# First stage of a convolution block: the generating vectors of its matrices are built with a group of channels on each partition

## The chip, the core and the metric

The kernel runs on one core of a Trainium2 chip. A core has five engines that run their own instruction queues side by side: TensorE (PE in the profile, with its weight loads listed as PEld), VectorE (DVE), ScalarE (ACT), GpSimd (POOL) and SyncE (SP), the last of which only issues transfers here. Transfers between DRAM and the on-chip memory run on 16 DMA engines. The metric is the device time of one execution in microseconds (us); the times given are medians of several executions.

## The reference, cut to what matters

The input is 16 images of 192 channels and 64 x 64 pixels, float32. Layer 0 normalizes over channels, projects to 384 channels, convolves half of them depthwise, runs four directional scans and a second depthwise convolution, gates, batch-normalizes and projects back; an MLP follows. Layer 1 is a depthwise convolution whose taps depend on the image.

```python
h = _ln2d(x, ln1_w, ln1_b)
pg = _conv1x1(h, in_proj_w, in_proj_b)
projected, gate = jnp.split(pg, 2, axis=1)
projected = _dwconv3(projected, dw_k)
scanned = _directional_scan(projected, decay_logits, mix_logits, input_scale)
local = _dwconv3(projected, le_k)
mixed = (scanned + local) * jax.nn.sigmoid(gate)
...
decay = jnp.clip(jax.nn.sigmoid(decay_logits), 0.05, 0.995)
mix = jax.nn.softmax(mix_logits, axis=0)
iscale = 1.0 + jnp.tanh(input_scale)
...
lr = _scan_axis(x * sc(iscale[0]), decay[0], -1)
```

The second stage of the kernel computes the depthwise convolutions and one axis of the scans as matrix products: for each channel it needs eight 64 x 64 Toeplitz matrices. Such a matrix is given by one vector of 127 numbers, its generating vector: the value depends on the difference of row and column only. Three vectors per channel (k = 0 to 2) hold the columns of `dw_k`, three (k = 3 to 5) those of `le_k`, one (k = 4) also the two exponential tails of the scans along that axis, and two (k = 6, 7) a single number, the gain of the scans along the other axis. The gain is softmax(mix) x (1 + tanh(input_scale)) x (1 - decay).

## The kernel before

Three stages follow each other. The first (to about 620 us) reads the images, normalizes them over channels and projects them; the second (to about 1,390 us) works channel by channel; the third runs the output projection, the MLP and layer 1.

The first stage runs 64 iterations `n`, each over a pair of images and eight rows. In iteration n, `load_a(n + 3)` issues the loads of a later input tile `xa`, three on SP's queue and three on POOL's (L471; four buffers). `store` (L536) and, at the start of a block, `store_first` (L530) issue the stores of the block before. PE then turns the next tile (12 transposes, L483) and runs the projection (24 products, L512, into two PSUM buffers per image). DVE and ACT each evict one half of the result (L517, L518), DVE takes the statistics of the next tile (L490, L491). Four iterations make a block. The evicted block lies in one of two buffers by turns, `stg` and `mid`, each there once. The stores of a block are spread over the four iterations of the next block, the last of them (`PARTS` entry 4, 192 KB each) issued in its fourth iteration; after that the block after next writes the same buffer again.

The order on every engine is the order of the program text. Small jobs are set beside the iterations: `beside(n, f, ...)` lists function f for the end of iteration n, behind that iteration's loads, stores, products and evictions on each engine.

The generating vectors are such small jobs. `decays` (before the loop) and `gains` (iteration 1) compute decay and gain with channels on 64 partitions in three parts (`dec`, `gain`: 64 x 3 x 4). For vector k, `vector(k)` on DVE clears a slot of 64 x 3 x 128 numbers and copies the few that are not zero; for k = 4, `runs(t)` in three iterations adds the exponential tails with a scan each. `positions(k)` turns the slot with three PE transposes into a PSUM bank (L403), which ACT copies to a tile `gt` with position on the partitions (L405). `store_vector(k, part)` writes it to DRAM, to `dv_d` (k < 3, two parts) or `lv_d` (four parts), each part in an iteration of its own, by turns on the queues of SP and POOL (L412, L416). In DRAM the layout is `dv_d[group][k][position][8 channels]` and `lv_d[group][half][k][position][4 channels]`, so a partition of `gt` is written in runs of 8 or 4 float32: 32 or 16 bytes. The vectors' iterations are 9, 11, 13, 15, 19, 24, 28 and 32; `positions` follows two later (five for k = 4), the parts one iteration after another behind it. From iteration 46 on `load_dm` and `load_lm` read the matrices back, each row of a matrix shifted by one position.

The slots and small tiles lie in the room of a weight tile `wf1` that is loaded in iteration 41 (`room`, `cut`).

Of the kernel before, what the change touches and what calls it, by code (L numbers as in the profile page):

```python
# [21 lines left out]
F32 = mybir.dt.float32  # L22
AF = mybir.ActivationFunctionType
ALU = mybir.AluOpType
# [31 lines left out]
def conv_block_kernel(ctx: ExitStack, tc: tile.TileContext, x, prm, w_in, w_out, w_fc1, b_fc1, w_fc2, w1, bn1, w2, out):  # L56
# [189 lines left out]
    with ExitStack() as stage:  # L246
# [11 lines left out]
        dcol, imp = cut(64, 1728, 64), cut(64, 1792, 64)  # L258
        indt, svt = cut(3, 1984, 128), cut(3, 2112, C)
        dec = ka.tile([64, 3, 4], F32, tag="dec", name="dec")  # L260
        gain = ka.tile([64, 3, 4], F32, tag="gain", name="gain")
        tmp = ka.tile([64, 3, 4], F32, tag="tmp", name="tmp")
        red = ka.tile([64, 3], F32, tag="red", name="red")
# [3 lines left out]
        gts = {}  # L267
# [19 lines left out]
        def decays():  # L287

            nc.scalar.activation(dec, pt3[lo, :, DEC:DEC + 4], AF.Sigmoid)
            nc.vector.tensor_scalar(dec, dec, 0.05, 0.995, ALU.max, ALU.min)  # L290
            nc.scalar.activation(tmp, pt3[lo, :, ISC:ISC + 4], AF.Tanh)
            nc.vector.tensor_scalar_add(tmp, tmp, 1.0)
            nc.vector.tensor_reduce(red, pt3[lo, :, MIX:MIX + 4], AX.X, ALU.max)
            for t in range(3):
                nc.vector.tensor_scalar(gain[:, t], pt3[lo, t, MIX:MIX + 4], red[:, t:t + 1], None, ALU.subtract)
            nc.scalar.activation(gain, gain, AF.Exp)

        def gains():
            nc.vector.tensor_reduce(red, gain, AX.X, ALU.add)
            nc.vector.reciprocal(red, red)  # L300
            nc.vector.tensor_mul(gain, gain, tmp)
            nc.vector.tensor_scalar(tmp, dec, -1.0, 1.0, ALU.mult, ALU.add)
            nc.vector.tensor_mul(gain, gain, tmp)
            for t in range(3):
                nc.vector.tensor_scalar_mul(gain[:, t], gain[:, t], red[:, t:t + 1])
# [69 lines left out]
        slot = lambda k: cut(64, 384 * (k % 2), 384).rearrange("p (t n) -> p t n", t=3)  # L375

        def vector(k):
            gv = slot(k)
            nc.vector.memset(gv, 0.0)
            if k < 3:  # L380
                nc.vector.tensor_copy(gv[:, :, 62:65], pt3[lo, :, DW + 3 * k:DW + 3 * k + 3])
            elif k < 6:
                le = pt3[lo, :, LE + 3 * (k - 3):LE + 3 * (k - 3) + 3]
                nc.vector.tensor_copy(gv[:, :, 62:65], le[:, :, ::-1])
            else:
                nc.vector.tensor_copy(gv[:, :, 63:64], gain[:, :, k - 4:k - 3])

        def runs(t):

            gv = slot(4)  # L390
            if t == 0:
                nc.vector.memset(imp, 0.0)
            for k, vec in ((0, gv[:, t, 63:127]), (1, gv[:, t, 63::-1])):
                run = cut(64, 1856 + 64 * k, 64)
                nc.vector.tensor_scalar_mul(dcol, ones[lo, 0:64], dec[:, t, k:k + 1])
                nc.vector.tensor_copy(imp[:, 0:1], gain[:, t, k:k + 1])
                nc.vector.tensor_tensor_scan(run, dcol, imp, 0.0, ALU.mult, ALU.add)
                nc.vector.tensor_add(vec, vec, run)

        def positions(k):  # L400
            pg = bank()
            for t in range(3):
                nc.tensor.transpose(pg[:, 64 * t:64 * t + 64], slot(k)[:, t], ident[lo, lo])  # L403
            gts[k] = ka.tile([128, C], F32, tag="gt", name="gt", bufs=4)
            nc.scalar.copy(gts[k], pg[:, 0:C])  # L405

        def store_vector(k, part):

            queue = (nc.sync, nc.gpsimd)[part % 2]
            if k < 3:  # L410
# [855 lines left out]
```

## Time and profile before

| | us |
|---|---|
| median of three executions | 3730.94 |
| lowest and highest of them | 3727.93, 3739.55 |
| the profiled execution | 3721.87 |
| span of the profiled execution, first to last instruction | 3720.1 |

| engine, whole span | busy us | share |
|---|---|---|
| PE | 3694.2 | 99% |
| DVE | 2699.1 | 73% |
| ACT | 1785.3 | 48% |
| POOL | 419.6 | 11% |

How to read the profile: a line of a timeline or of a group names the line of the kernel (L512), the engine, the operation and "output<-input", then how often. What stands in brackets, or after a bar, is the time for which the engine sat idle before it, and what released it. SPq and ACTq are those engines as issuers of transfers; POOL's transfers stand under POOL. The releaser of a wait for several things is inferred, and can be the wrong one of them. DMA shares are means over the 16 engines. Matmuls are pipelined and their ends are modelled, so a busy PE is not a PE at its peak: the distance from one start to the next says more than the busy share.

### The profile page before, as it was taken

What the parts mean: (1) busy time and instruction counts of PE and PEld (TensorE: products, weight loads), DVE (VectorE), ACT (ScalarE), POOL (GpSimd) and SP (SyncE); (2) the same over time, 40 slices, a digit from 0 to 9 for tenths busy, and PEclk for the clock granted to TensorE, in tenths of its full rate; (3) what the DMA queues carried; (4) which work ended last, traced back from release to release, by engine and by line L of the source; (5) the groups of instructions that cost most, each with busy time, mean ns of one, the idle gap of its engine ahead of it and who ended that gap; (6) DMA issues with size and microseconds to landing.
All of it is one profiled execution on the core that took longest, in us unless ns stands there. A gap on an engine that the chain in (4) does not pass through costs nothing.

```text
span 3720.1 us, 71189 instructions
## 1 busy us (share of the span) xinstructions
PE 3694.2 (99%) x30344; PEld 1644.7 (44%) x30344; DVE 2699.1 (73%) x4154; ACT 1785.3 (48%) x1947; POOL 419.6 (11%) x683
## 2 busy tenths in 40 slices
PE   9999999999999999999999999999999999999999
PEld 6665666555555533333333333333333333333333
DVE  7887776999999965557757757666765766675763
ACT  3443444888888843334434433434343443443433
POOL 2434332101111020000000000000000000000000
PEclk9999999999999999999999999999999999999999
DMA  7899997999999851112212222222222221221212
GB/s 169 243 249 233 269 286 248 302 293 283 280 285 271 233 101 36 42 44 69 79 50 69 71 65 68 63 63 65 72 57 60 75 71 44 78 75 44 69 38 74
DMA packets 310236, 491.76 MB, mean 132 GB/s; under 512 B 46672, under 2 KB 204704, under 8 KB 309920
## 3 DMA queue, kind: packets, MB, share of 16 engines
q1 hardware_dynamic: 252128, 296.19, 29.8%
q0 software_dynamic: 56896, 189.89, 18.9%
q8 instruction: 240, 3.93, 0.5%
q10 hardware_dynamic: 896, 1.12, 0.1%
q14 instruction: 76, 0.62, 0.1%
HBM read 284.91 MB, written 197.92 MB: 130 GB/s over the span
## 4 chain that ended last, share of the span: by engine, by line
PE 98%; DVE 1%; DMA 1%; ACT 0%; issue 0%; SPq 0%; POOL 0%; ACTq 0%
PE ps_f L981 27%; PE ps_f L835 27%; PE ps_pj L512 14%; PE ps_l L669 11%; PE ps_d L625 7%; PE ps_o L906 5%; PE ps_xt L483 2%; PE ps_o L899 2%; PE ps_o L937 1%; DMA xa<-in_x_dram 0%; PE ps_k L835 0%; PE ps_d L1068 0%; PE ps_i L1109 0%; DVE v L662 0%; DVE v L660 0%; DMA pg_d<-mid 0%
## 5 line engine op out<-in xcount | busy, mean ns | idle before, releaser
L983 ACT ACTIVATE gl<-ps_f,bf 128x1024 f32<-128x1024 f32 x384 | 427.6, 1114 | 1319.2 <-PE ps_f L981 1319.2
L981 PE MATMUL ps_f<-h,wf 64*64 64x512 f32 x9216 | 1033.3, 593 | 3.0 <-DVE h L969 1.8
L835 PE MATMUL ps_f<-gl,place 128*64 128x512 f32 x4608 | 1022.2, 592 | 0.0
L981 PEld LDWEIGHTS ps_f<-h,wf 64*64 64x64 f32 x9216 | 333.6, 133 | 688.4 <-issue 633.7
L835 PEld LDWEIGHTS ps_f<-gl,place 128*64 128x64 f32 x4608 | 334.2, 137 | 574.5 <-issue 533.4
L512 PE MATMUL ps_pj<-wi,xa 64*128 64x384 f32 x3072 | 515.4, 488 | 2.9 <-DVE stg L517 2.9
L949 DVE TENSOR_TENSOR h<-ximg,ps_o 128x768 f32<-128x768 f32 x126 | 114.5, 950 | 420.9 <-PE ps_o L906 412.6
L512 PEld LDWEIGHTS ps_pj<-wi,xa 64*128 64x128 f32 x3072 | 294.4, 187 | 195.4 <-issue 12.2
L912 DVE SCALAR_TENSOR_TENSOR ximg<-ps_o,pt,low 128x256 f32<-128x256 f32 x384 | 167.8, 479 | 262.7 <-PE ps_o L906 259.1
L65 DVE SCALAR_TENSOR_TENSOR o<-ximg,taps,o 128x1024 f32<-128x1024 f32 x261 | 334.7, 1282 | 9.3 <-ACT o L1040 2.6
L1044 POOL DMA_DIRECT2D out_dram<-o x168 | 87.9, 528 | 2067.5 <-DVE o L65 2064.7
L968 DVE RECIPROCAL rs<-rs 128x512 f32<-128x512 f32 x64 | 214.3, 3349 | 28.6 <-ACT rs L965 28.6
L660 DVE TENSOR_TENSOR_SCAN v<-tab,q 128x1024 f32<-128x1024 f32 x96 | 218.3, 2274 | 7.8 <-ACT tab L648 7.8
L662 DVE TENSOR_TENSOR_SCAN v<-tab,q 128x1024 f32<-128x1024 f32 x96 | 217.4, 2265 | 0.0
L648 ACT ACTIVATE tab<-mask,dec_b 128x1024 f32<-128x1024 f32 x192 | 209.4, 1142 | 0.0
L906 PE MATMUL ps_o<-low,wo 128*64 128x256 f32 x1536 | 209.0, 393 | 0.0
L518 ACT ACTIVATE stg<-ps_pj,rsa 128x384 f32<-128x384 f32 x128 | 120.0, 941 | 184.2 <-PE ps_pj L512 168.8
L518 ACT ACTIVATE mid<-ps_pj,rsa 128x384 f32<-128x384 f32 x128 | 119.9, 938 | 182.1 <-PE ps_pj L512 178.4
L490 DVE BATCH_NORM_STATS2 st<-ps_xt 128x6 f32<-128x192 f32 x512 | 173.0, 338 | 14.4 <-PE ps_xt L483 14.2
L239 DVE STREAM_TRANSPOSE low<-low 128x512 f32<-128x512 f32 x174 | 167.7, 1014 | 2.0 <-issue 0.3
L1001 DVE SCALAR_TENSOR_TENSOR ximg<-ps_f,pt,ximg 128x512 f32<-128x512 f32 x192 | 134.4, 749 | 40.2 <-PE ps_f L835 37.8
L471 POOL DMA_DIRECT2D xa<-in_x_dram x192 | 119.9, 630 | 354.8 <-PE ps_pj L512 284.3
(211 smaller groups left out, 4047.2 us busy)
## 6 DMA issues: line engine op xcount, KB each, us to landing
low<-in_x_dram SPq DMA_DIRECT2D x128, 384.0 KB
out_dram<-o POOLq DMA_DIRECT2D x168, 256.0 KB, 3.7
mid<-pg_d SPq DMA_DIRECT2D x8, 4096.0 KB
low<-mixed_d SPq DMA_DIRECT2D x116, 256.0 KB
low<-pg_d SPq DMA_DIRECT2D x7, 4096.0 KB
pg_o<-pg_d SPq DMA_DIRECT2D x7, 4096.0 KB
xa<-in_x_dram POOLq DMA_DIRECT2D x192, 128.0 KB, 5.9
xa<-in_x_dram SPq DMA_DIRECT2D x192, 128.0 KB
```

The costliest lines, as they stand in the source:

```text
L65: nc.vector.scalar_tensor_tensor(o, in0, scalar, in1, ALU.mult, ALU.add, **kw)
L512: nc.tensor.matmul(ps[i], pixels(n, t, g)[q], wi[q, t].rearrange("p g k c -> p (g k c)"), start=(t == 0), stop=(t == 2))
L518: nc.scalar.activation(stag[blk][1][:, :, j], ps[1], AF.Copy, scale=rs[:, g, 1:2])
L625: nc.tensor.matmul(dst(ps[o, ih]), mats[g % 2]["dm"][q, di + 1, :, ch], src(s["pg"][q, :, 0, ch]), start=(di == 0), stop=stop)
L660: nc.vector.tensor_tensor_scan(vf, tab, q, 0.0, ALU.mult, ALU.add)
L662: nc.vector.tensor_tensor_scan(vf[:, ::-1], tab[:, ::-1], q[:, ::-1], 0.0, ALU.mult, ALU.add)
L669: nc.tensor.matmul(dst(bst[k]["ps"][o, i]), lm_of(g)[q, m, :, c], src(q, ih), start=start, stop=stop)
L835: nc.tensor.matmul(ps[q], w(i), rhs(i), start=start, stop=stop)
L906: nc.tensor.matmul(ps[wh][q].rearrange("p (r w) -> p r w", w=32), wo[:, 64 * t:64 * t + 64], cols(rows(s["mx"][:, i]))[:, :, wh], start=fi ...
L968: nc.vector.reciprocal(rs, rs)
L981: nc.tensor.matmul(pf[o, i], wf1[q, t, m0:m0 + 64], s["h"][q, t], start=(t == 0), stop=(t == 2))
L983: nc.scalar.activation(gl, pf, AF.Gelu, bias=bf1[:, m:m + 1])
```

## The change

The vectors are built with one group of eight channels on each of 24 partitions, each partition holding all 128 positions in the order in which DRAM has them. The parameters are loaded a second time for this, as `ptg` (24 x 8 x 50, issued by ACT before the loop). `group_gains` computes decay and gain from it in that layout (part 0 before the loop, part 1 in iteration 1); `decays` keeps only the decay that `diagonals` needs, and `gains` is gone. A slot is 24 x 1024 numbers, on partitions 64 to 87 or 96 to 119. POOL clears it, DVE copies the numbers that are not zero, and for k = 4 `runs(i, d)` makes the exponential tails, in four iterations, with one scan over 256 numbers each. `positions` is gone: there are no transposes, no copies by ACT and no `gt`. `store_vector` writes a vector with one transfer: `dv_d` on SP's queue in runs of 4 KB, `lv_d` on POOL's queue in runs of 2 KB. The vectors' iterations are now 13, 14, 15, 16, 24, 32, 33, 34, with the store one iteration later (five for k = 4).

```diff
--- before.py
+++ after.py
@@ -255,16 +255,11 @@
         dg = cut(64, 768, 576).rearrange("p (t k n) -> p t k n", t=3, k=3)
         lnb = cut(64, 1344, 384).rearrange("p (t n) -> p t n", t=3)
         mean_w = cut(64, 0, 128)
-        dcol, imp = cut(64, 1728, 64), cut(64, 1792, 64)
         indt, svt = cut(3, 1984, 128), cut(3, 2112, C)
         dec = ka.tile([64, 3, 4], F32, tag="dec", name="dec")
-        gain = ka.tile([64, 3, 4], F32, tag="gain", name="gain")
-        tmp = ka.tile([64, 3, 4], F32, tag="tmp", name="tmp")
-        red = ka.tile([64, 3], F32, tag="red", name="red")
         bp = ka.tile([64, 3], F32, tag="bp", name="bp")
         sv = ka.tile([64, 3, 3, 3], F32, tag="sv", name="sv")
         ind = ka.tile([128, 3], F32, tag="ind", name="ind")
-        gts = {}
 
         def bank():
             return psa.tile([128, CH], F32, tag="pb", name="pb")
@@ -288,21 +283,6 @@
 
             nc.scalar.activation(dec, pt3[lo, :, DEC:DEC + 4], AF.Sigmoid)
             nc.vector.tensor_scalar(dec, dec, 0.05, 0.995, ALU.max, ALU.min)
-            nc.scalar.activation(tmp, pt3[lo, :, ISC:ISC + 4], AF.Tanh)
-            nc.vector.tensor_scalar_add(tmp, tmp, 1.0)
-            nc.vector.tensor_reduce(red, pt3[lo, :, MIX:MIX + 4], AX.X, ALU.max)
-            for t in range(3):
-                nc.vector.tensor_scalar(gain[:, t], pt3[lo, t, MIX:MIX + 4], red[:, t:t + 1], None, ALU.subtract)
-            nc.scalar.activation(gain, gain, AF.Exp)
-
-        def gains():
-            nc.vector.tensor_reduce(red, gain, AX.X, ALU.add)
-            nc.vector.reciprocal(red, red)
-            nc.vector.tensor_mul(gain, gain, tmp)
-            nc.vector.tensor_scalar(tmp, dec, -1.0, 1.0, ALU.mult, ALU.add)
-            nc.vector.tensor_mul(gain, gain, tmp)
-            for t in range(3):
-                nc.vector.tensor_scalar_mul(gain[:, t], gain[:, t], red[:, t:t + 1])
 
         def diagonals(t):
             for k, v in enumerate((pt3[lo, t, GTB:GTB + 1], dec[:, t, 2:3], dec[:, t, 3:4])):
@@ -372,49 +352,69 @@
             by_half(bias_q[:, k], pq[:, 0:C])
 
 
-        slot = lambda k: cut(64, 384 * (k % 2), 384).rearrange("p (t n) -> p t n", t=3)
+
+        GP = slice(64, 64 + NCG)
+        ptg = ka.tile([128, GC, NPRM], F32, tag="ptg", name="ptg")[GP]
+        decg, gaing, tmpg = (ka.tile([128, GC, 4], F32, tag=n_, name=n_)[GP] for n_ in ("decg", "gaing", "tmpg"))
+        redg = ka.tile([128, GC], F32, tag="redg", name="redg")[GP]
+        NV = 128 * GC
+        slots = (room[GP, 0:NV], room[96:96 + NCG, 0:NV])
+        HN = GC // 2 * HW
+        dcol, imp, run = (room[GP, NV + k * HN:NV + (k + 1) * HN].rearrange("g (c m) -> g c m", m=HW) for k in range(3))
+        by_pair = lambda v: v.rearrange("g (i c) n -> g i n c", i=2)
+        slot = lambda k: slots[k % 2].rearrange("g (i s c) -> g i s c", i=2, c=GC // 2)
+
+        def group_gains(part):
+
+            mix = ptg[:, :, MIX:MIX + 4]
+            if part == 0:
+                nc.scalar.activation(decg, ptg[:, :, DEC:DEC + 4], AF.Sigmoid)
+                nc.scalar.activation(tmpg, ptg[:, :, ISC:ISC + 4], AF.Tanh)
+                nc.vector.tensor_scalar(decg, decg, 0.05, 0.995, ALU.max, ALU.min)
+                nc.vector.tensor_scalar_add(tmpg, tmpg, 1.0)
+                nc.vector.tensor_reduce(redg, mix, AX.X, ALU.max)
+                nc.vector.tensor_sub(gaing, mix, redg.unsqueeze(2).broadcast_to([NCG, GC, 4]))
+                nc.scalar.activation(gaing, gaing, AF.Exp)
+            else:
+                nc.vector.tensor_reduce(redg, gaing, AX.X, ALU.add)
+                nc.vector.reciprocal(redg, redg)
+                nc.vector.tensor_mul(gaing, gaing, tmpg)
+                nc.vector.tensor_scalar(tmpg, decg, -1.0, 1.0, ALU.mult, ALU.add)
+                nc.vector.tensor_mul(gaing, gaing, tmpg)
+                nc.vector.tensor_mul(gaing, gaing, redg.unsqueeze(2).broadcast_to([NCG, GC, 4]))
 
         def vector(k):
-            gv = slot(k)
-            nc.vector.memset(gv, 0.0)
+            nc.gpsimd.memset(slots[k % 2], 0.0)
             if k < 3:
-                nc.vector.tensor_copy(gv[:, :, 62:65], pt3[lo, :, DW + 3 * k:DW + 3 * k + 3])
-            elif k < 6:
-                le = pt3[lo, :, LE + 3 * (k - 3):LE + 3 * (k - 3) + 3]
-                nc.vector.tensor_copy(gv[:, :, 62:65], le[:, :, ::-1])
+                nc.vector.tensor_copy(slots[k % 2].rearrange("g (s c) -> g s c", c=GC)[:, 62:65],
+                                      ptg[:, :, DW + 3 * k:DW + 3 * k + 3].rearrange("g c j -> g j c"))
+                return
+            for i in range(2):
+                gv, c = slot(k)[:, i], slice(i * (GC // 2), (i + 1) * (GC // 2))
+                if k < 6:
+                    le = ptg[:, c, LE + 3 * (k - 3):LE + 3 * (k - 3) + 3]
+                    nc.vector.tensor_copy(gv[:, 62:65], le[:, :, ::-1].rearrange("g c j -> g j c"))
+                else:
+                    nc.vector.tensor_copy(gv[:, 63:64], gaing[:, c, k - 4:k - 3].rearrange("g c j -> g j c"))
+
+        def runs(i, d):
+
+            gv, c = slot(4)[:, i], slice(i * (GC // 2), (i + 1) * (GC // 2))
+            nc.vector.memset(imp, 0.0)
+            nc.vector.tensor_copy(imp[:, :, 0:1], gaing[:, c, d:d + 1])
+            nc.vector.memset(dcol[:, :, 0:1], 0.0)
+            nc.vector.tensor_copy(dcol[:, :, 1:HW], decg[:, c, d:d + 1].broadcast_to([NCG, GC // 2, HW - 1]))
+            flat = lambda v: v.rearrange("g c m -> g (c m)")
+            nc.vector.tensor_tensor_scan(flat(run), flat(dcol), flat(imp), 0.0, ALU.mult, ALU.add)
+            vec = gv[:, 63:127] if d == 0 else gv[:, 63::-1]
+            nc.vector.tensor_add(vec, vec, run.rearrange("g c m -> g m c"))
+
+        def store_vector(k):
+            if k < 3:
+                nc.sync.dma_start(dv_d[:, k].rearrange("g s c -> g (s c)"), slots[k % 2])
             else:
-                nc.vector.tensor_copy(gv[:, :, 63:64], gain[:, :, k - 4:k - 3])
-
-        def runs(t):
-
-            gv = slot(4)
-            if t == 0:
-                nc.vector.memset(imp, 0.0)
-            for k, vec in ((0, gv[:, t, 63:127]), (1, gv[:, t, 63::-1])):
-                run = cut(64, 1856 + 64 * k, 64)
-                nc.vector.tensor_scalar_mul(dcol, ones[lo, 0:64], dec[:, t, k:k + 1])
-                nc.vector.tensor_copy(imp[:, 0:1], gain[:, t, k:k + 1])
-                nc.vector.tensor_tensor_scan(run, dcol, imp, 0.0, ALU.mult, ALU.add)
-                nc.vector.tensor_add(vec, vec, run)
-
-        def positions(k):
-            pg = bank()
-            for t in range(3):
-                nc.tensor.transpose(pg[:, 64 * t:64 * t + 64], slot(k)[:, t], ident[lo, lo])
-            gts[k] = ka.tile([128, C], F32, tag="gt", name="gt", bufs=4)
-            nc.scalar.copy(gts[k], pg[:, 0:C])
-
-        def store_vector(k, part):
-
-            queue = (nc.sync, nc.gpsimd)[part % 2]
-            if k < 3:
-                n = NCG // 2
-                queue.dma_start(dv_d[part * n:part * n + n, k].rearrange("g s c -> s g c"),
-                                  gts[k].rearrange("s (g c) -> s g c", c=GC)[:, part * n:part * n + n])
-            else:
-                n = NCG // 4
-                queue.dma_start(lv_d[part * n:part * n + n, :, k - 3].rearrange("g i s c -> s (g i) c"),
-                                  gts[k].rearrange("s (g c) -> s g c", c=GC // 2)[:, 2 * part * n:2 * part * n + 2 * n])
+                nc.gpsimd.dma_start(lv_d[:, :, k - 3].rearrange("g i s c -> g i (s c)"),
+                                    slots[k % 2].rearrange("g (i n) -> g i n", i=2))
 
 
         side = {}
@@ -422,7 +422,7 @@
         def beside(n, f, *args):
             side.setdefault(n, []).append((f, args))
 
-        beside(1, gains)
+        beside(1, group_gains, 1)
         for t in range(3):
             beside(2 + t, diagonals, t)
         beside(5, gate_bias)
@@ -434,15 +434,12 @@
         for k in range(3):
             beside(18 + 2 * k, sums_across, k)
             beside(19 + 2 * k, conv_bias, k)
-        for k, n in enumerate((9, 11, 13, 15, 19, 24, 28, 32)):
+        for k, n in enumerate((13, 14, 15, 16, 24, 32, 33, 34)):
             beside(n, vector, k)
             if k == 4:
-                for t in range(3):
-                    beside(n + 1 + t, runs, t)
-            end = n + (5 if k == 4 else 2)
-            beside(end, positions, k)
-            for part in range(2 if k < 3 else 4):
-                beside(end + 1 + part, store_vector, k, part)
+                for j in range(4):
+                    beside(n + 1 + j, runs, j // 2, j % 2)
+            beside(n + (5 if k == 4 else 1), store_vector, k)
         for k in (0, 1, 3, 4):
             beside(40 + k, load_weights, k)
         for i in range(2):
@@ -541,6 +538,7 @@
             v = src.rearrange("(t p) n -> p t n", p=64)
             nc.sync.dma_start(dst[HALF[0]], v)
             nc.scalar.dma_start(dst[HALF[1]], v)
+        nc.scalar.dma_start(ptg, prm.rearrange("(g c) n -> g c n", c=GC))
         nc.vector.memset(ones, 1.0)
 
         idle = bank()
@@ -558,6 +556,7 @@
         steps = projection_weights()
         next(steps)
         decays()
+        group_gains(0)
         next(steps)
         next(steps)
         turn(0)
```

## The prediction

> **What bounds the kernel now.** The page comes first: the engines' shares say which engine sets the time, the chain which of its lines.
>
> ```profile
> PE 3694.2 (99%) x30344; PEld 1644.7 (44%) x30344; DVE 2699.1 (73%) x4154; ACT 1785.3 (48%) x1947; POOL 419.6 (11%) x683
> ...
> DMA  7899997999999851112212222222222221221212
> ...
> DMA packets 310236, 491.76 MB, mean 132 GB/s; under 512 B 46672, under 2 KB 204704, under 8 KB 309920
> ...
> PE 98%; DVE 1%; DMA 1%; ACT 0%; issue 0%; SPq 0%; POOL 0%; ACTq 0%
> ```
>
> PE is the chain, and the DMA engines are full in the first 14 slices, the first stage among them. Work taken from DVE, ACT or a queue counts only where PE waits for it. So the second view is the timeline of PE over three iterations, of which the middle one has no transposes of a vector:
>
> ```profile
> 133.37 0.34 PE L403 MATMUL pb<-ident,wf 64*128 64x64 f32 x3
> 133.64 1.53 PE L483 MATMUL ps_xt<-ident,xa 128*128 128x128 f32 x12
> 135.10 8.01 PE L512 MATMUL ps_pj<-wi,xa 64*128 64x384 f32 x48
> 143.04 1.53 PE L483 MATMUL ps_xt<-ident,xa 128*128 128x128 f32 x12
> ```
>
> From one L483 to the next it is 143.04 - 133.64 = 9.40 us, and the same in nearly every iteration to 604 us: PE runs at its own pace, though the DMA engines are full. I listed all 62 distances for what stands above 9.40. The eight iterations with L403 take 9.57 or 9.58. The jobs of other kinds (L315 to L371) take theirs and stay. Three are not explained by PE's work: 9.71 from 114.35, 9.86 from 443.36, and one of 15.05 from 324.73 us. The timeline there (all engines), and SP's own before it:
>
> ```profile
> 305.89 13.19 SPq L471 DMA_DIRECT2D xa<-in_x_dram  x3
> 319.12 2.13 SPq L536 DMA_DIRECT2D pg_d<-stg  x2
> 321.42 3.32 SPq L471 DMA_DIRECT2D xa<-in_x_dram  x3
> 324.79 1.30 SPq L536 DMA_DIRECT2D pg_d<-stg  x2
> 326.39 0.37 SPq L416 DMA_DIRECT2D lv_d<-gt  x1
> ...
> 332.98 1.58 ACT L518 ACTIVATE stg<-ps_pj,rsa 128x384 f32<-128x384 f32 x2 [7.13 <-DMA pg_d<-mid]
> 333.11 0.86 DVE L517 TENSOR_SCALAR stg<-ps_pj,rsa 128x384 f32<-128x384 f32 x1 [4.93 <-DMA pg_d<-mid]
> ...
> 334.02 5.84 PE L512 MATMUL ps_pj<-wi,xa 64*128 64x384 f32 x24 [2.86 <-DVE stg L517]
> ```
>
> A new block begins there (iteration 32), and its first evictions write `stg`. They wait until the last store of the block that lay in it has landed. The profile names a store from `mid`, but what is overwritten is `stg`; its last store left SP only at 324.79 to 326.09, 7 us before. It was late because SP was late: its three loads of 305.89 took 13.19 us to issue. DVE and ACT stand, both PSUM buffers fill, and PE waits 2.86 us. The 24 products after that take 5.84 us instead of 4.14: the page by windows gives PE a granted clock of 0.91 in 320 to 340 us and 1.00 on either side.
>
> Around that time the vectors' stores stand in both queues. Each moves 96 or 48 KB in 1,536 runs of 32 or 16 bytes:
>
> ```profile
> L416 SPq DMA_DIRECT2D lv_d<-gt x10: 366/1452/2260, 199.2 to 388.2; - x10
> L416 POOL DMA_DIRECT2D lv_d<-gt x10: 1034/1075/1077, 203.3 to 391.3; - x10
> ...
> L412 SPq DMA_DIRECT2D dv_d<-gt x3: 1327/1563/2089, 142.6 to 179.5; - x3
> ...
> DMA to landing us min/median/max: 6.5/9.6/12.0
> ```
>
> Six in `dv_d` and 20 in `lv_d` make 26 x 1,536 = 39,936 packets, of 46,672 under 512 B in the whole execution. In 277 to 296 us, with two of them on SP and two on POOL, the DMA engines moved 184 GB/s at a share of 0.95; in 454 to 473 us, with none, 274 at 0.89.
>
> **What the Trainium skill says.** "DMA: Bandwidth & Descriptors", section Specifications: a transfer needs runs of 512 B or more for the full rate, and below that the engine reads, modifies and writes. The 184 against 274 GB/s agree. The same page, "Issuing engines are not separate DMA queues": all queues run on the same 16 engines, so POOL's small stores hold up SP's loads too; SP's 13.19 us fits this. "TensorE: Matmul & The Clock Gate", Part 1: after an idle window of some 3.4 us PE's clock is halved until it has been busy as long again. The trace agrees in kind: 2.86 us of waiting, with gaps just ahead of it, cost 15.05 - 9.40 = 5.65 us.
>
> **The change, part by part.**
>
> *Transposes.* Eight times 0.17 to 0.18 us by the distances above (0.27 us from L403 to L483, less what the L403 overlap with the products): -1.4 us, all on PE's path. This is sure.
>
> *ACT's eight copies* of 306 ns go: nothing, ACT is idle half of the iteration.
>
> *The stores.* 39,936 packets become 3 x 24 of 4 KB and 5 x 48 of 2 KB, 312 in all, with the same bytes; 13 transfers leave SP's queue and 3 come, 13 leave POOL's and 5 come. SP, loaded like this, is in time elsewhere: from iteration 10 to 12, before the first of these stores, its loads are issued at 114.48, 124.20 and 133.60, beside PE's 114.35, 124.06 and 133.64. So I expect the wait at iteration 32 to go, -5.65 us. Bounds: 0 if the full DMA engines alone made it, and more than 5.65 where an execution has it at several blocks. That it is chance which blocks are hit, the trace suggests: at iteration 16, beside the `dv_d` stores, ACT waited 2.54 us for a transfer in the same place, and PE did not feel it.
>
> *DVE's jobs.* A vector loses its memset (378 ns). The tails now cost, in each of iterations 25 to 28: a memset of 256 (0.28, between 112 ns for 64 and 378 for 384), two tiny ones (0.20), a copy of 252 (0.36, as L318 for 192), a scan of 256 (283 ns for 64 and 2,270 for 1024 give 0.68) and an addition of 256 (217 ns for 64, some 1 ns each more: 0.42): 1.94 us. DVE's fixed work is 8 x 0.47 (statistics) + 4 x 0.89 + 0.20 = 7.5 of 9.4 us, so 1.9 us are free. Before, `runs` took 2 x 0.88 = 1.75 us, in iteration 21 with 0.46 of `conv_bias`, and the period there (9.92) was that of iteration 23 without `runs`. So nothing; at most 4 x 0.1 us.
>
> *POOL's memset* of 1024 numbers: 170 ns for 64 and 200 for 128 (L113, masks) give some 0.6 us by their slope; I take 1 and bound it by 10, as no row shows a long one. POOL is free 2 to 6 us of each iteration (its waits for PE ahead of L471), so its loads and stores aren't late. DVE's copies wait for the memset, and behind them stand the next statistics and evictions; but the copy is due at the end of the iteration and POOL is done with its transfers 3 to 6 us into it. For k = 2 and 3 the memset also waits until the store of k - 2 has landed, issued an iteration earlier; with landings of 6.5 to 12 us that is 2 to 8 us into the iteration. Nothing, with 1 to 5 us of cover.
>
> *The start.* `ptg` is ACT's third transfer, behind 295 KB of weights that land at 8.3 us; `group_gains(0)` stands on DVE ahead of L284. Before, those small jobs ended at 10.1, L284 began at 11.72 and ended at 13.2, and PE needed it only at 15.23, after the wait for the first tile (to 14.64). So `ptg` may land up to 11 us for nothing and costs at most some 2 us if it lands with the tile. I take 0.
>
> *Sum:* 3721.87 - 1.4 - 5.65 = 3714.8 us against the profiled execution's own time. The three timed ones stand 6 to 18 us above it. One, two or three more waits of 5.65 us would give 3727.5, 3733.2 and 3738.8; two of the three (3727.93, 3739.55) lie near, which proves nothing but fits. If so, the changed kernel loses these too. I leave 1 us for what else a timed run has.
>
> **The rivals.** A measurement tells 0.3%, 11.2 us here, from no change: the bound is at 3719.7 us.
>
> 1. The waits go in every execution: 3716 us. Chance 0.54.
> 2. What lifts the timed runs by 9.07 us is something else, and stays: 3730.94 - 7.05 = 3723.9, no measurable change. For it: no profile shows a timed run. Chance 0.27.
> 3. The bytes fill the DMA engines, not the packets, and the block wait stays: the shares without these stores are as high (1.06 in 500 to 519 us). Only 1.4 us go: 3729.5. Against it: no such wait after 400 us, bar the 9.86. Chance 0.08.
> 4. Slower: DVE stands behind POOL's memset. It decides once memset, queue and landing end 9.4 + 1.9 = 11.3 us into the iteration, that is from memsets of some 7 us, or from a landing after 10 us. At the bound of 10 us, DVE is held some 2 us at eight places, each with PE's clock behind it (2 more, as at 334 us), 32 us in all: 3723.9 + 32, less what overlaps, some 3745. Against it: both memsets of POOL in the trace run near 1 ns a number or less. Chance 0.11.
>
> **How the numbers follow.** The forecast is the first: 3716 us. Faster by over 0.3% has the chance 0.54, within it 0.27 + 0.08 = 0.35, slower 0.11. The range reaches over cases 2 and 3 and leaves out most of 4: up to 3731, and down to 3709, where the timed runs lose both the waits and the residue of other block starts.
>
> **What would show it.** Right: no L403; periods of 9.40 in the eight iterations; none above 10 us between 130 and 600; packets under 512 B near 6,700; SP's loads issued within 2 us of PE's start around iteration 30. Wrong: DVE waiting at the copies for POOL, L284 ending after 15 us, or a wait of the evictions for a store at the start of a block.

## The result, and the profile after

| | before | after |
|---|---|---|
| median of six executions each, us | 3732.44 | 3718.85 |
| lowest and highest, us | 3727.93, 3739.55 | 3717.61, 3720.48 |
| the profiled execution, us | 3721.87 | 3717.9 |
| span of the profiled execution, us | 3720.1 | 3716.1 |

The ratio is 0.9971, with a 95% interval of 0.9961 to 0.9982: faster by 0.29%, about the 0.3% that the prediction called the bound of what can be told from no change. The two rows that stand on a profile differ by 4.0 us only, the medians by 13.6. This gap is taken up below, since it decides how much of the result is the change's.

The page of the changed kernel, the same lines as before: engines, DMA by slices, packets, and now its queues (packets, MB, share of the 16 engines).

```profile
PE 3693.1 (99%) x30320; PEld 1649.0 (44%) x30320; DVE 2700.6 (73%) x4147; ACT 1784.8 (48%) x1940; POOL 419.1 (11%) x683
...
DMA  7898997999999841112312222222222221221212
...
DMA packets 289820, 491.80 MB, mean 132 GB/s; under 512 B 26456, under 2 KB 184144, under 8 KB 289504
...
q1 hardware_dynamic: 232060, 296.09, 29.4%
q0 software_dynamic: 56512, 189.99, 18.5%
```

PE lost 24 instructions (the transposes), and is the chain as before. The packets fell by 20,416, not by the 39,600 that the prediction counted. Nearly all of it is the queue q1, on which SP's transfers lie: 252,128 to 232,060, or 13 x (1,536 + 16) less 3 x (24 + 12), exactly the 13 small-run transfers that left SP and the three that came, if each of those also has 16 and 12 packets of its own. POOL's queue q0 fell from 56,896 by 384 only. What POOL issued in short runs was never counted as a packet for each run, though the bytes were there: its 384 packets are 8 x 48, and 8 transfers fewer left it. A transfer of 1,536 runs moves 48 KB in `dv_d` and 24 KB in `lv_d`, as the list of transfers has it; the prediction's 96 and 48 are twice that.

The stage itself, by the timeline of PE. First where the prediction had the wait, with SP's queue:

```profile
293.35 1.53 PE L480 MATMUL ps_xt<-ident,xa 128*128 128x128 f32 x12
...
303.04 1.53 PE L480 MATMUL ps_xt<-ident,xa 128*128 128x128 f32 x12
...
312.44 1.53 PE L480 MATMUL ps_xt<-ident,xa 128*128 128x128 f32 x12
```

```profile
303.25 6.61 SPq L468 DMA_DIRECT2D xa<-in_x_dram  x3
...
312.58 2.61 SPq L468 DMA_DIRECT2D xa<-in_x_dram  x3
315.23 1.27 SPq L533 DMA_DIRECT2D pg_d<-stg  x2
```

SP's loads begin 0.2 us after PE's transposes (303.25 beside 303.04, 312.58 beside 312.44), take 6.61 us where they took 13.19, and the last stores of the block leave at 315.23 instead of 324.79; the turn of iteration 30 itself began 2.7 us earlier (303.04 beside 305.75). The periods after it are 9.40; the 15.05 is gone. In 277 to 296 us the windows show a DMA share of 0.76 with 207 GB/s, for 0.95 with 184 before.

Two things came that the prediction did not have. On PE, while DVE makes the tails:

```profile
273.67 1.53 PE L480 MATMUL ps_xt<-ident,xa 128*128 128x128 f32 x12
275.13 8.29 PE L509 MATMUL ps_pj<-wi,xa 64*128 64x384 f32 x48
283.35 1.53 PE L480 MATMUL ps_xt<-ident,xa 128*128 128x128 f32 x12
284.81 4.14 PE L509 MATMUL ps_pj<-wi,xa 64*128 64x384 f32 x24
289.28 4.14 PE L509 MATMUL ps_pj<-wi,xa 64*128 64x384 f32 x24 [0.33 <-DVE mid L514]
```

The four periods from 264.22 us are 9.45, 9.68, 10.00 and 9.69: 1.22 us more than 4 x 9.40. What stands on DVE in one of them:

```profile
275.18 0.27 DVE L403 MEMSET wf<- 24x256 f32 x1
...
275.57 0.49 DVE L406 COPY wf<-decg 24x252 f32<-24x252 f32 x1
...
276.09 0.68 DVE L408 TENSOR_TENSOR_SCAN wf<-wf 24x256 f32<-24x256 f32 x1
276.81 0.59 DVE L410 TENSOR_TENSOR wf<-wf 24x256 f32<-24x256 f32 x1
277.43 0.37 DVE L487 BATCH_NORM_STATS2 st<-ps_xt 128x6 f32<-128x192 f32 x1
```

From 275.18 to 277.40 is 2.2 us without a gap, and the statistics and evictions behind it follow without a gap too. DVE was full. The third of the four periods, 10.00 us, also has a wait of 0.42 us in it, of DVE for a store at the start of a block (to 288.37).

And at the start of the block at iteration 44, by the timelines of SP, PE and ACT:

```profile
427.41 7.66 SPq L468 DMA_DIRECT2D xa<-in_x_dram  x3
435.50 1.13 SPq L533 DMA_DIRECT2D pg_d<-mid  x2
```

```profile
435.62 1.50 PE L480 MATMUL ps_xt<-ident,xa 128*128 128x128 f32 x12 [0.91 <-DMA xa<-in_x_dram]
437.05 4.14 PE L509 MATMUL ps_pj<-wi,xa 64*128 64x384 f32 x24
441.78 5.01 PE L509 MATMUL ps_pj<-wi,xa 64*128 64x384 f32 x24 [0.59 <-DVE mid L514]
```

```profile
441.70 1.63 ACT L515 ACTIVATE mid<-ps_pj,rsa 128x384 f32<-128x384 f32 x2 [5.91 <-DMA w1t<-in_w_dram]
```

It is the wait of iteration 32 again, in another place: SP is late (here behind the loads of the later stages' weights, L116 and L70, L71 from 407 us on), the last stores from `mid` leave at 435.50, and the first evictions of the next block, which write `mid`, wait. ACT stood 5.91 us; the named releaser, a load of weights, is only the last transfer before it. Three periods, from 425.24, 435.62 and a third four turns later, are 10.38, 11.10 and 9.78 us: 3.06 us over 9.40. Before had 0.46 there.

From the second turn to the last turn of the first stage the two traces take 593.72 and 590.16 us (19.30 to 613.02, 16.74 to 606.90). The terms: -1.41 for the eight transposes, -5.65 for the wait, -0.31 for the long turn from 114.35 us, +1.22 for the tails, +2.60 for the weights' block: -3.55, and it is -3.56. The long turn is no chance: it takes 9.70 to 9.72 us in all six traces that keep the old vectors, and 9.40 in all eight that have the new ones. Before, DVE does the tap sums and then clears and fills vector 0 there (115.66 to 118.24 us), and its evictions follow late; now vector 0 is begun four iterations later. That this is the reason was not tested alone. The rest of the difference in span doesn't come from these steps: the second turn began 2.56 us sooner, and the 36 small matmul records after the stage (L140) took 6.25 us for 4.61, at the same wait ahead of them. (PE's list shows each float32 product as two records, so x24 are 12 products.)

### The profile page after: what moved, and what is told of

Its sections match the earlier page's. It is cut to its first block, busy times and chain, and to the rows that moved or that the text cites. A ratio compares the mean times of both kernels' runs of the same rounds, so it can differ in the third digit from the quotient of the medians.

```text
span 3716.1 us, 71125 instructions
## 1 busy us (share of the span) xinstructions
PE 3693.1 (99%) x30320; PEld 1649.0 (44%) x30320; DVE 2700.6 (73%) x4147; ACT 1784.8 (48%) x1940; POOL 419.1 (11%) x683
## 3 DMA queue, kind: packets, MB, share of 16 engines
q1 hardware_dynamic: 232060, 296.09, 29.4%
## 4 chain that ended last, share of the span: by engine, by line
PE 90%; DVE 1%; DMA 1%; ACT 0%; SPq 0%; issue 0%; POOL 0%; ACTq 0%; DVEq 0%
PE ps_f L980 27%; PE ps_f L834 27%; PE ps_l L668 11%; PE ps_pj L509 7%; PE ps_d L624 7%; PE ps_o L905 5%; PE ps_o L898 2%; PE ps_o L936 1%; PE ps_xt L480 1%; DMA xa<-in_x_dram 0%; PE ps_k L834 0%; PE ps_d L1067 0%; PE ps_i L1108 0%; DVE v L661 0%; PE pb_h L140 0%; DVE v L659 0%
```

## The experiments

The theory: the short runs of the vectors' stores make SP's issuing late, SP's lateness makes the last store of a block late, and that makes the evictions of iteration 32 wait. Rivals: the bytes or the full DMA engines make the wait whatever the runs (rival 3 of the prediction); the gain is the set of executions and not the change (rival 2); what DVE or the transposes do moves the times. Each kernel was timed beside the kernel before on the same chip; the four sets ran on four chips. Each run has one trace, of one execution out of 10 to 21.

### The kernel before, again

> The kernel before, unchanged, for a second look at its trace. Theory A (chance waits of the evictions for a late store at the start of a block, behind the vectors' stores of 16 and 32 byte runs): in iterations 12 to 40 one to three periods of PE above 10 us, not all at the iteration of the first trace (32), and a time of 3716 plus some 5 us for each; the ratio to before is 1.000. Theory B (what lifts the timed executions above the first profiled one lies elsewhere): again one such period or none, and any excess over 3722 us stands after 620 us.

14 executions beside 44 of the kernel before: 3725.28 us against 3724.3, ratio 1.0006 (0.9996 to 1.0017), as it must be. The wait is there, in the same place, and at no other block up to iteration 40, where theory A expected some. It is 8.63 us this time, of which 2.11 are PE's wait for the late input tile itself, one iteration earlier:

```profile
303.13 13.87 SPq L471 DMA_DIRECT2D xa<-in_x_dram  x3
```

```profile
333.19 1.59 ACT L518 ACTIVATE stg<-ps_pj,rsa 128x384 f32<-128x384 f32 x2 [10.05 <-DMA pg_d<-mid]
...
334.24 5.83 PE L512 MATMUL ps_pj<-wi,xa 64*128 64x384 f32 x24 [2.90 <-DVE stg L517]
```

### Long runs in another layout

```diff
-    dv_d = dram.tile([NCG, 3, 128, GC], ...)
+    dv_d = dram.tile([3, NCG, 128, GC], ...)
...
-                queue.dma_start(dv_d[part * n:part * n + n, k].rearrange("g s c -> s g c"), ...)
+                queue.dma_start(dst.rearrange("(p n) -> p n", n=C)[p], gts[k][p])
```

> The kernel before with one thing undone: the vectors are stored by the same 26 transfers, in the same iterations and queues and with the same bytes, but each partition's part in one run of 768 bytes, so the values stand in DRAM in another order and the matrices are not those of the reference. Transposes, copies by ScalarE and all jobs of VectorE stay. Theory A: no period above 10 us in iterations 12 to 40, a time of 3719 to 3723 us (the changed kernel's 3718.9, plus 1.4 us for the transposes, less 1.2 us for the tails that are cheaper here), and a spread of 3 to 5 us in place of 11. Theory B (the gain is not that of the runs' length): 3730 us or more, like before.

3730.88 us (15), ratio 1.0015 (1.0007 to 1.0023): slower, the time of theory B. The trace has no wait at iteration 32, and the first stage from its second turn takes 589.34 us, 4.4 less than before. What was gained there is lost in the second stage, by PE's timeline:

```profile
737.18 4.54 PE L623 MATMUL ps_d<-pg_o,dm 64*64 64x512 f32 x40 [2.09 <-DMA dm<-dv_d]
...
879.76 2.90 PE L623 MATMUL ps_d<-low,dm 64*64 64x512 f32 x40 [2.77 <-DMA dm<-dv_d]
```

The loads of the matrices now gather planes that lie far apart in DRAM, and PE waits for them. So the run tells of the wait, but its time is that of two edits at once. The experiment was repeated without the new layout below.

### The small runs put back into the changed kernel

```diff
+        def store_small(k, part):
+            queue = (nc.sync, nc.gpsimd)[part % 2]
+            if k < 3:
+                n = NCG // 2
+                queue.dma_start(dv_x[part * n:part * n + n, k].rearrange("g s c -> s g c"), ...)
...
+        for k, n in enumerate((9, 11, 13, 15, 19, 24, 28, 32)):
+            end = n + (5 if k == 4 else 2)
+            for part in range(2 if k < 3 else 4):
+                beside(end + 1 + part, store_small, k, part)
```

> The changed kernel with the suspected cost put back alone: 26 more transfers, with runs of 32 and 16 bytes, in the iterations and queues of the kernel before, from a tile of zeros to a scratch area of DRAM that nothing reads. No transposes, no copies by ScalarE. Theory A: the waits come back, one to three periods above 10 us in iterations 12 to 40, a time of 3727 to 3737 us with a spread of some 10 us. Theory B: 3719 to 3721 us.

3726.23 us (20), ratio to the kernel before 1.0006 (0.9999 to 1.0012): the gain is gone. The wait is back where it was, on SP, ACT and PE (the lines shown stand 20 lower down in this kernel than in the changed one):

```profile
307.62 11.47 SPq L488 DMA_DIRECT2D xa<-in_x_dram  x3
```

```profile
334.04 1.63 ACT L535 ACTIVATE stg<-ps_pj,rsa 128x384 f32<-128x384 f32 x2 [7.01 <-DMA pg_d<-mid]
...
335.08 7.12 PE L529 MATMUL ps_pj<-wi,xa 64*128 64x384 f32 x24 [3.59 <-DVE stg L534]
```

Its period is 16.25 us. A second wait of the same kind stands twelve turns earlier, at the start of the block of iteration 20, whose period is 12.46 us where the other kernels but one have 9.56:

```profile
216.31 3.81 PE L529 MATMUL ps_pj<-wi,xa 64*128 64x384 f32 x21 [1.20 <-ACT mid L535]
```

Nothing else of before came back, neither transposes nor copies. It has 0.8 MB more to store, though, so this alone doesn't separate runs from bytes; the next does.

### The same stores in long runs, in place

```diff
-                queue.dma_start(dv_d[part * n:part * n + n, k].rearrange("g s c -> s g c"),
-                                  gts[k].rearrange("s (g c) -> s g c", c=GC)[:, part * n:part * n + n])
+                queue.dma_start(dv_d[g, k].rearrange("g s c -> g (s c)"), filler[g])
```

> The kernel before with its 26 stores in their iterations and queues, in runs of 4 and 2 KB from a cleared tile, into the same places of DRAM as before: the matrices are zero, so the output is not the reference's. Transposes, copies by ScalarE and VectorE's jobs stay. The first try stored into another layout, and the second stage then waited for its matrices. Theory A: no wait at iteration 32, none for matrices in the second stage, 1 to 2 us above the changed kernel (1.4 for the transposes, less the 1.2 of the tails, plus what its first tile costs). Theory C (the changed kernel gains by leaving out transposes, copies or DVE's jobs, not by the runs): the time of the kernel before.

3715.88 us (17), ratio 0.9981 (0.9974 to 0.9988). The same 26 transfers with the same number of bytes, from the same queues in the same iterations, and the wait is gone. SP's loads of that iteration:

```profile
304.23 5.31 SPq L471 DMA_DIRECT2D xa<-in_x_dram  x3
...
312.25 2.70 SPq L471 DMA_DIRECT2D xa<-in_x_dram  x3
```

The transposes' turns of 9.57 are still there, and none of the tails on 24 partitions is. So it is the runs and not the bytes: rival 3 falls, and the gain doesn't need the transposes to go. Zeros are stored here in place of the vectors, so what it would cost to bring these into DRAM's order in another way isn't in this time. The time is 3.5 us below the changed kernel's of the same set (3719.39), where 1 to 2 us above it was expected. Why stays open: the profiled executions are only 0.5 us apart (3716.9 and 3717.41). In them the turns of the first stage take 0.9 us more here, and the second turn began 4.2 us sooner (16.24 beside 20.46).

### The small runs on one queue alone

```diff
+                if part % 2 == 0:
+                    beside(end + 1 + part, store_small, k, part)
```

(SP's 13 transfers; for POOL's 13 the remainder is 1.)

> The changed kernel with the half of the finely cut scratch stores that SP issued (13 of the 26), none on POOL's queue. In all traces with the short runs SP's three loads of iteration 30 took 11.5 to 13.9 us to issue, after iterations 27 and 28 in which two vectors' stores fell together, and the wait stood at iteration 32. If SP's own ring is what fills: three loads of 11 us or more there again, and the period above 14 us at iteration 32. If the work of both queues on the shared 16 DMA engines is what counts: half of it is let through, loads of 4 to 8 us, no period above 10 but the known ones.

> As before, with the 13 scratch stores on POOL's queue alone. If SP's own ring fills: no wait at iteration 32. If the shared engines count: the same half as with SP's, neither or both have the wait.

3718.39 us (18) with SP's, ratio 0.9988 (0.9981 to 0.9995); 3718.73 (16) with POOL's, 0.9991 (0.9984 to 0.9999). Neither has the wait; SP's three loads of iteration 30 took 6.53 us with SP's and 5.72 with POOL's:

```profile
308.90 6.53 SPq L489 DMA_DIRECT2D xa<-in_x_dram  x3
```

```profile
303.89 5.72 SPq L489 DMA_DIRECT2D xa<-in_x_dram  x3
```

So neither the 13 issues on SP as such nor POOL's alone make SP this late. It takes more than either half. Whether it is the two queues or the number of runs isn't shown, since 26 such transfers on one queue were not run.

### The kernel before, with its vectors further apart

In the kernel before, the stores of vectors 4 and 5 fall together in iterations 27 and 28, two of them on each queue. Moving the last three vectors two iterations back each takes them apart:

```diff
-        for k, n in enumerate((9, 11, 13, 15, 19, 24, 28, 32)):
+        for k, n in enumerate((9, 11, 13, 15, 19, 26, 30, 34)):
```

> The kernel before with the vectors 5, 6 and 7 begun two iterations later (26, 30, 34 in place of 24, 28, 32), so that no two vectors' stores fall into one iteration; all runs stay 32 and 16 bytes. If two vectors' stores at once are what fills the queues: no wait at iteration 32, 5 to 8 us less than before. If any finely cut store near the end of a block is enough: the wait stays or moves to iteration 36.

3718.18 us (12), ratio 0.9994 (0.9985 to 1.0003), which tells nothing by itself and doesn't show the 5 to 8 us expected. In the trace the wait at iteration 32 shrinks from the 4.7 to 8.6 us of the other traces to 1.2 (all above 9.40), at the same count of runs in the execution:

```profile
308.35 6.86 SPq L471 DMA_DIRECT2D xa<-in_x_dram  x3
```

```profile
330.42 4.14 PE L512 MATMUL ps_pj<-wi,xa 64*128 64x384 f32 x24 [0.75 <-DVE stg L517]
```

These 24 records took 4.14 us after a wait of 0.75, and 5.83 to 5.84 after the waits of 2.78 to 2.90 in the three traces of before.

A wait stands at iteration 20 too, 1.05 us over the usual 9.56. The edit doesn't reach that place, and the stores ahead of it are those of single vectors:

```profile
214.89 4.14 PE L512 MATMUL ps_pj<-wi,xa 64*128 64x384 f32 x24 [0.78 <-DVE mid L517]
```

So two vectors at once are not needed for a wait. Why this trace and the one with the small runs put back wait there, and the three of before don't, isn't shown.

### The changed kernel, twice more, and before once more

> The changed kernel, unchanged, on the chip of its neighbours here. Theory A (the vectors' short runs made the wait at iteration 32 and a part of the spread): 3717 to 3720 us, spread some 3 us, no PE period above 10 us in iterations 12 to 40 but the tails' (1.2 us in all over iterations 26 to 29); ratio to before 0.997 to 0.999. Theory B (the difference was between two sets of executions, not two kernels): the same median as before within 1 us.

> The changed kernel on the chip of its neighbours here: the ratio to before, which was 0.997 on one chip and 0.999 on another, once more. If the gain is the one wait, less what the tails cost, and the rest is the spread of the executions: 3 to 8 us, ratio 0.998 to 0.999.

> The kernel before, a third trace. If the wait at iteration 32 belongs to the program and not to chance: three loads of SP in iteration 30 that take over 11 us, and periods of PE at iterations 31 and 32 that are together 5 to 9 us too long. If it is chance: it stands elsewhere or is absent.

The changed kernel took 3719.39 us (13) beside 3722.83 of before (48), ratio 0.9989 (0.9981 to 0.9997); on another chip 3718.9 (21) beside 3721.54 (63), 0.9990 (0.9983 to 0.9996). Its tails cost 1.00 and 1.23 us, its weights' block 2.72 and 3.05. The kernel before, on the fourth chip, was level with itself (3722.56 for 3721.2, ratio 1.0004, 0.9994 to 1.0014), with a profiled span of 3714.3 us, shorter than any of the changed kernel's; and still it has the wait, 4.74 us of it, behind three loads of 10.99 us on SP:

```profile
331.25 5.83 PE L512 MATMUL ps_pj<-wi,xa 64*128 64x384 f32 x24 [2.78 <-DVE stg L517]
```

So one execution's time says little here, and the wait at iteration 32 shows in all three traces of before and in none of the three of after.

### The weights' loads spread out, and the tails in halves

```diff
-        for k in (0, 1, 3, 4):
-            beside(40 + k, load_weights, k)
+        for k, n in ((0, 39), (1, 43), (5, 47), (3, 51), (4, 55)):
+            beside(n, load_weights, k)
...
-        beside(50, squeeze_scale)
+        beside(59, squeeze_scale)
```

> The changed kernel with the loads of the second stage's weights (iterations 40 to 44) spread over iterations 39, 43, 47, 51 and 55, the large one in two halves, each behind the last store of a block. Theory A' (any large or finely cut transfer ahead of the last store of a block makes the same wait): the periods of 10.38 and 11.10 us at iterations 43 and 44 go, 2.5 us less than the changed kernel, also in the times. Theory B': the loads only move the wait to another iteration, no change within 1 us.

> As the kernel before this one in the list, and the tails' jobs on VectorE cut in two, over eight iterations (24 to 31) in place of four: 0.9 and 1.3 us where VectorE has some 1.9 us free, not 2.2. If the tails overload VectorE, the periods of iterations 24 to 31 are all 9.40 us and 1.2 us less than with the weights alone; if they don't, nothing.

In the second, each of the four tails is also split over two iterations (the memsets and copies in one, scan and addition in the next), from iteration 24 to 31. 3716.05 us (15) and 3717.14 (14) beside the changed kernel's 3719.39 of the same set; ratio to before 0.9981 (0.9973 to 0.9988) for both. With the weights moved every turn from 425 to 480 us is 9.40. PE's timeline of the second, where DVE makes the tails:

```profile
266.49 1.53 PE L483 MATMUL ps_xt<-ident,xa 128*128 128x128 f32 x12
...
275.89 1.53 PE L483 MATMUL ps_xt<-ident,xa 128*128 128x128 f32 x12
...
285.29 1.53 PE L483 MATMUL ps_xt<-ident,xa 128*128 128x128 f32 x12
```

9.40 in each. These are the best of the versions whose vectors are whole. The executions don't tell the two apart, and their intervals overlap that of the changed kernel; by the traces the first stage from its second turn takes 586.7 and 585.9 us for the changed kernel's 589.5 to 590.2.

### All traces together

Microseconds above 9.40 a turn, added up from PE's timelines: at the tails and the transposes beside them, at iteration 32, and at the weights' block; then the whole from the second turn to the last.

| kernel | tails | iteration 32 | weights | stage |
|---|---|---|---|---|
| before, three traces | 0.34 to 0.35 | 5.65, 8.63, 4.74 | 0.46, 1.24, 0.00 | 593.7, 597.5, 592.3 |
| after with the small runs on both queues | 0.92 | 6.85 | 0.00 | 596.6 |
| before, vectors apart | 0.18 | 1.19 | 0.79 | 590.5 |
| before, long runs, other layout | 0.35 | 0.00 | 1.77 | 589.3 |
| before, long runs in place | 0.35 | 0.00 | 2.73 | 590.4 |
| after with SP's small runs; POOL's | 0.96; 0.73 | 0.00 | 1.92; 2.56 | 588.8; 589.2 |
| after, three traces | 1.22, 1.00, 1.23 | 0.00 | 3.06, 2.72, 3.05 | 590.2, 589.5, 590.0 |
| after, weights moved | 0.99 | 0.00 | 0.00 | 586.7 |
| and tails in halves | 0.00 | 0.00 | 0.00 | 585.9 |

The wait at iteration 20 is in no column but the last: 2.90 us over the usual 9.56 with the small runs put back, 1.05 with the vectors apart.

The columns of iteration 32 and of the weights go against each other: every kernel that waits 4.7 us or more at iteration 32 loses at most 1.24 us at the weights' block, and every one that doesn't wait loses 1.8 to 3.1 there, unless the weights are moved. A part of the gain is given back twelve iterations later. That PE, no longer held up, arrives there with the same bytes still to be moved is the reading that suggests itself; the runs show the trade, not this cause.

## Why the prediction was right, and where it was not

The forecast of 3716 us, faster, is 2.85 us below the 3718.85 measured. That the number came so near is in part luck. The steps that it read from the trace add up to 7.05 us, and the first stage shows a gain of 3.55; most of the rest of the 13.6 us is what lifted the kernel before in that set, which is not explained (last step below). Its steps:

- *Transposes*: -1.4 us forecast, -1.41 measured. ACT's copies: nothing, as said.
- *The stores*: the mechanism is what was shown. Long runs alone take the wait away (long runs in place), short runs alone bring it back. -5.65 was the size in that trace; 4.74 and 8.63 in the others. That chance decides which blocks are hit was only half right. In all three traces of before, and with the runs put back, the large wait stands at iteration 32, where the stores of two vectors have met in iterations 27 and 28, ahead of that block's last stores; taken apart, they leave 1.2 us. But the block of iteration 20 waits in two of the five traces with short runs on both queues and not in the other three, and its size varies at iteration 32 too: there chance has its part.
- *What is late next* was not asked of the later iterations, and so the gain forecast for the stage was 2.6 us too large. The step said that SP "is in time elsewhere", from a stretch before the first small store; at the weights' loads it is not, and 2.7 to 3.1 us come back there. The sign that it named, no period above 10 us up to 600, did not come: 10.38 and 11.10 stand there.
- *Packets*: 39,936 to 312 was the arithmetic of runs. The trace's count fell by 20,416, as it never had POOL's runs; "near 6,700 under 512 B" was wrong by 20,000, while the mechanism didn't depend on it.
- *DVE's tails*: forecast at nothing, at most 0.4 us; 1.00 to 1.23. The term that was mis-sized is the addition: 0.42 us, with 1 ns a number assumed, against 0.594 measured. Its operand is strided here, which may be why; no run tests it. The groups by form, mean ns of one after the comma:

```profile
L408 DVE TENSOR_TENSOR_SCAN wf<-wf 24x256 f32<-24x256 f32 x4 | 2.7, 682 | 0.1
L410 DVE TENSOR_TENSOR wf<-wf 24x256 f32<-24x256 f32 x4 | 2.4, 594 | 0.1
L406 DVE COPY wf<-decg 24x252 f32<-24x252 f32 x4 | 1.5, 382 | 0.0
```

  The scan's 0.68 was right, and the copy's 0.36 on the mean (0.27 and 0.49 by turns). So one job takes 2.0 or 2.2 us, against 1.9 free; the four periods are 0.05 to 0.60 us too long, and the largest has the block's wait in it. With the tails halved they are 9.40, so the tails are what costs. Having worked out 1.94 for a gap of 1.9, the prediction should not have called it nothing.
- *POOL's memset*: 1 us taken, 0.946 measured, hidden; rival 4 falls, its point of decision was 7 us. In POOL's groups by form the addition to its queue is as small:

```profile
L387 POOL MEMSET wf<- 24x1024 f32 x8 | 7.6, 946 | 0.3
L416 POOL DMA_DIRECT2D lv_d<-wf x5 | 3.1, 614 | 1.0 <-issue 1.0
```

- *The start*: nothing was forecast, and the first pair of traces shows no cost. `ptg` was there for ACT at 7.84 us, and DVE had done what it makes of it before L279 could begin, at 11.21 behind PE. PE's second turn began at 16.74. But over the fourteen traces it begins at 16.2 to 19.3 us in the six without `ptg` (17.6 on average) and at 16.7 to 21.2 in the eight with it (19.3), after waits for input tiles. So a cost of some 1 to 2 us is not excluded; no run tests it.
- *From the profile to the timed runs*: the forecast explained before's 9 us above its profile by one to three more such waits. No trace shows an execution with two or three of them at full size, and in the experiments' four sets the kernel before has medians of 3721.2 to 3724.3 us, at its profile. There the change is worth 0.1% (3.4 and 2.6 us of medians, in the two sets that have it), near the sum of what the turns of the first pair of traces show (-3.55). In this sense rival 2 was nearer: most of the first set's 13.6 us isn't in the mechanism. What lifted before in that set was not in any trace, and stays open. Before's executions do spread more (3716 to 3737 us in those sets) than the 34 of the changed kernel (3716 to 3724), and those with short runs put back on both queues reach 3732; so waits of varying size may be part of it, but that was not seen.

The forecast sum of 3714.8 for the profiled execution met 3717.9. The 3.1 us between are the tails (1.22) and the weights' block (2.60), less the long turn (0.31) and what the start and the products of L140 gave and took.

## What to carry to other kernels

When an engine waits at a block's start for a buffer, follow the last store of the block that lay in it back through its queue. Here small transfers of 1,536 short runs each, issued 20 to 45 us earlier on two queues, made it late. Longer runs with the same bytes took the wait away, and spacing took most of it. A wait that is removed upstream in a stage with full DMA engines can come back at the next burst of loads, as 2.6 us may have done here after 5.65 were gained, so look there before counting the gain. And where a change is worth 0.1%, one profile and six executions can't size it: compare the same places in several traces, and take the medians of sets on several chips.

## What was not expected of the hardware

- PE's clock after a short wait. The 36 records of L140 follow a wait of 1.03 to 1.12 us and took 4.17 to 6.80 us in traces of kernels that don't differ there. The windows give a granted clock of 0.64 and then 0.67 in 625 to 632 and 632 to 640 us of the changed kernel; before, where the records run from 631.34 us, they give 0.89 in 631 to 636 and 0.68 in 632 to 640. So the clock falls in both, in one while the records run and in the other behind most of them. "TensorE: Matmul & The Clock Gate", Part 1, in the Trainium skill, says that the window over which PE's activity is judged runs freely, so the cost varies from run to run. The spread agrees. The page's idle window of some 3.4 us can't be checked here: the wait was 1.1 us, but the records behind it have one column each, and how busy they count isn't shown.
- Two halves that are harmless alone. The skill's page "DMA: Bandwidth & Descriptors", in "Issuing engines are not separate DMA queues", has all queues share 16 engines. The runs agree: 13 transfers of 1,536 short runs on either queue left SP's loads of iteration 30 at 5.7 to 6.5 us, 26 on both made them 11.0 to 13.9, and 26 on both with the vectors apart 6.9.
- With another layout of the 0.8 MB of vectors, planes far apart in place of side by side, PE waited 2.1 and 2.8 us for loads with the same bytes at the places shown; no other trace has such a wait there.
